# Feed-forward steps and next-sequence preparation moved half a slot to a slot later in hand-written engine orders

## The chip, the cores and the metric

The kernel runs on one core of one Trainium2 chip. A core has five engines that each work through their own list of instructions in order: PE (TensorE, matrix products and transposes), DVE (VectorE), ACT (ScalarE), POOL (GpSimd) and SP (SyncE, which here only issues transfers). Semaphores make an instruction wait for others, and what stands behind a waiting instruction on the same engine waits too. The metric is the device time of the execution in microseconds (us). Before the change it was 1479.51 us, the median of three runs (1479.34 to 1482.35).

## The reference

The input `x` is 8 sequences of 512 tokens with 256 features. The program is one transformer block:

```
x = x + layernorm(attention(layernorm(x)))
x = x + layernorm(ffn(layernorm(x)))
```

Attention has 16 query heads of width 128 in 4 groups; each group shares one key and one value head. Queries and keys get a sinusoidal position added; scores are causal and scaled by 1/sqrt(128); the heads' outputs are multiplied by `wo` (2048 x 256). The feed-forward part is a mixture of 64 experts (width 176). A token's gate scores are a softmax over 64 logits, its six best experts are taken, each expert takes at most 64 tokens in the order in which they come, and the outputs are summed with the scores as weights. A shared expert of width 352 is added for every token. All of it is fp32.

```
logits = x @ gate_w.T;  scores = softmax(logits);  topk_w, topk_idx = top_k(scores, 6)
g = silu(buf @ w_gate);  u = buf @ w_up;  d = (g * u) @ w_down        # per expert, 64 rows each
y = sum_k topk_w * d[...]  +  (silu(h @ sh_gate.T) * (h @ sh_up.T)) @ sh_down.T
```

## The kernel before

**Slots.** The main loop (from L903) runs over `k` from 0 to 127: sequence `b = k // 16`, head `s = k % 16`. One pass is called a slot here, "slot 4 of sequence 2" for `b = 2, s = 4`. The whole body runs under a manual schedule: every engine executes its instructions in the order in which the Python code emits them. A slot emits, in this order: the scores of head `k` (four row tiles, `scores`, each followed on DVE by a reduction called `least` that reads the score tile out of PSUM, and on ACT by an exponential); between the second and the third, `turned(k - 1)`, six DVE block transposes whose result goes through DRAM (`eb` to `ex_d` to `et`, issued by SP); then `weigh` (a DVE reciprocal, then four POOL multiplications of the softmax rows); place A; `project(k - 3)`; place B; `queries(k + 1)` (four PE pieces, and on DVE `qt`, which the next slot's scores need); `mix(k - 2)`; and place D.

**Places.** `side(s, place)` emits what a dictionary holds for that slot and place. The dictionary `behind` is filled at the end of slot 2 by `feed_forward(b - 1)`: it carries the second half of the block for the sequence just finished. Its steps that matter here are `copies` (attention output out of PSUM, ACT), `scales` (four `bn_stats`, four `bn_aggr`, one add on DVE, then a power on POOL), `residual_sums` (four DVE normalisations `o`, L106, then four POOL additions into `x`, L740), `store` (SP writes `x` to `x1_d`, L743), `rows` (four DVE normalisations into `xg`, L106), and `turn` (eight PE transposes `pt_f`, L119, whose two results are copied out by ACT and by DVE). Then come the shared expert (`shared_gate`, L681, with its DVE products L692 and L693) and the routing (`gate`, then `go("r")`: a reciprocal and eight small DVE operations, L392 to L398, in place D of slot 8).

**The next sequence.** `prepare(b + 1)` yields twelve units: the load of `x` (SP, L144), its scales, its normalisation `xn`, its transposes `pt_a` with the copies `xnt`, four `keys` units (PE `pk`, DVE `kt`) and four `values` units (PE `pv`, DVE add). One unit is emitted behind place D of a slot, and one slot has another just before `queries`.

**Buffers.** `ps_s` has three PSUM buffers, which score tiles and transposes (`psc`, `pt_f`, `pt_a`) take in turn; the fourth score tile takes the buffer of the first. Two transposes behind the scores of a slot take those of its second and third score tile, and the next slot's second and third score tile take the transposes'. `ps_m` has three for everything else. `x` has two buffers, so the load of sequence `b + 1` takes the one of sequence `b - 1`, which is free when `store` has landed and `rows` is done. `eb` has one.

**Experts.** Sequences 0 to 4 leave rows and gate scores in DRAM. From slot 14 of sequence 5 to about slot 4 of sequence 7 the generator `experts` (`routed`) runs the 32 pairs of experts between the attention steps: POOL gathers rows (`gx`, L513) and adds results into DRAM (`y_d`, L585), ACT's queue loads the weights (`wgu`, `wd`).

The places are called from these two lines, and nothing is reordered afterwards:

```
        def side(s, place):
            behind.pop(f"{s}{place}", lambda: None)()
```

Of the kernel before, what the change touches and what calls it, by code (L numbers as in the profile page):

```python
# [20 lines left out]
B, T, E = 8, 512, 256  # L21
# [18 lines left out]
EARLY = 5  # L40
# [4 lines left out]
def sandwich_kernel(ctx, tc, x, wq, bq_t, wkv, bk_t, bv, wo, gate_wt, w_gate, w_up, w_down,  # L45
# [26 lines left out]
    def norm_scales(tiles, name):  # L72

        n = len(tiles)
        st = small.tile([P, n, 6], F32, tag="st", name=f"st_{name}")
        for i in range(n):
            nc.vector.bn_stats(st[:, i, :], tiles[i])
        return scales_of(st, n, name)
# [20 lines left out]
    def tiles_of(t):  # L99
        return [t[:, i, :] for i in range(NI)]  # L100

    def rows_of(d, first):
        return d[first : first + T, :].rearrange("(i p) e -> p i e", p=P)

    def normalize(dst, src, mv, rs, i):
        nc.vector.tensor_scalar(dst, src, mv[:, i, 0:1], rs[:, i : i + 1], ALU.subtract, ALU.mult)  # L106
# [16 lines left out]
    with ExitStack() as part:  # L123
# [77 lines left out]
        turn = wpool.tile([1, NM], F32, tag="turn", name="turn")  # L201
# [70 lines left out]
        def queries(k):  # L272
            b, h = divmod(k, NH)
            pq = ps_m.tile([P, T], F32, tag="m", name=f"pq_{k}")
            for c in range(NC):
                nc.tensor.matmul(pq, lhsT=wq_sb[h // QPG][:, c, ts(h % QPG, D)], rhs=seqs[b]["xnt"][:, c, :],  # L276
                                 start=c == 0, stop=c == NC - 1)
            qt = p2.tile([D, T], F32, tag="qt", name=f"qt_{k}")
            nc.vector.scalar_tensor_tensor(qt, pq, bq_sb[:, h : h + 1], pe_sb, ALU.add, ALU.add)  # L279
            live[k] = {"qt": qt, "e": []}  # L280
# [383 lines left out]
        def residual(b, q, tag):  # L664
            x1 = q.tile([P, NI, E], F32, tag=tag, name=f"x1_{b}")
            nc.sync.dma_start(out=x1, in_=rows_of(x1_d, b * T))
            return x1
# [53 lines left out]
        def feed_forward(b):  # L721


            xt, sums = seqs[b]["x"], po.pop(b)
            l = {}

            def copies():
                l["o"] = p1.tile([P, NI, E], F32, tag="xn", name=f"o_{b}")
                for n in range(2):
                    nc.scalar.copy(l["o"][:, ts(n, 2), :], sums[n])  # L730

            def scales(src, name):
                l["scales"] = norm_scales(tiles_of(src), f"{name}{b}")

            def residual_sums():
                mv, rs = l.pop("scales")
                for i in range(NI):
                    normalize(l["o"][:, i, :], l["o"][:, i, :], mv, rs, i)
                for i in range(NI):
                    nc.gpsimd.tensor_add(xt[:, i, :], xt[:, i, :], l["o"][:, i, :])  # L740

            def store():
                nc.sync.dma_start(out=rows_of(x1_d, b * T), in_=xt)  # L743

            def rows():
                mv, rs = l.pop("scales")
                l["xg"] = p1.tile([P, NI, ROW], F32, tag="xg", name=f"xg_{b}")
                for i in range(NI):
                    normalize(l["xg"][:, i, :E], xt[:, i, :], mv, rs, i)

            def turn():
                l["xt2"] = p1.tile([P, NC, T], F32, tag="xt2", name=f"xt2_{b}")
                transpose_rows(l["xt2"], l["xg"], f"f{b}")

            def gate():
                l["r"] = route(b, l["xg"], l)
                next(l["r"])

            def shared_gate():
                l["f"] = shared(b, l["xt2"], l, "mmmmss" if b == B - 2 else "mmmmmm")  # L760
                next(l["f"])

            def go(which, n=1):
                return lambda: [next(l[which]) for _ in range(n)]

            steps = {
                "2D": copies, "3B": lambda: scales(l["o"], "o"), "3D": residual_sums,
                "4D": lambda: scales(xt, "f"), "5A": store, "5B": rows,
                "6A": turn, "7A": shared_gate, "7B": go("f"), "8A": gate,
                "8D": go("r"), "9D": go("r"),  # L770
            }
            if b < B - 2:
                steps |= {"9A": go("f"), "9B": go("f"), "11A": go("f"), "11B": go("f")}
            if b < EARLY:
                return steps | {"10A": go("r"), "10D": go("r", 2),
                                "11D": go("r", 2), "12A": go("f"), "12D": go("r", 2), "13A": go("f"), "13D": go("r", 2)}

            def mark():
                l["marks"] = marks(table["m"], l["xg"][:, :, E:ROW], table["places"], b, p1, "y")

            def gather_rows():
                gather("late", [(l["xg"], l["marks"][0])])
                l["gt"] = turn_scores(l.pop("marks")[1], b, *((p1, "xn") if b == EARLY else (p2, "kt", 5)))

            def begin_output():
                x1 = residual(b, p1, "xn") if b == EARLY else xt
                l["out"] = output(b, l["y"], x1)
                next(l["out"])

            def down_late():  # L790
                down("late")
                l["dd"] = pairs["late"]["dd"]

            steps |= {
                "10A": go("r"), "10B": mark, "10D": gather_rows, "11D": lambda: gate_up("late"),
                "12A": lambda: gate_up_hidden("late"), "12D": lambda: turn_hidden("late"), "13A": down_late,
            }
            if b < B - 2:
                return steps | {"13B": go("f"), "13D": lambda: [next(l["f"]), begin_output()],
                                "14B": go("out"), "15A": go("out")}  # L800

            steps["shared"], steps["output"] = go("f"), lambda: next(l["out"]) if "out" in l else begin_output()
            return steps
# [93 lines left out]
        behind, ahead = {}, iter(())  # L897
# [4 lines left out]
        def side(s, place):  # L902
            behind.pop(f"{s}{place}", lambda: None)()  # L903
            if not b:
                for u in rest.get(f"{s}{place}", ()):
                    u()

        for k in range(NK):
            b, s = divmod(k, NH)
            active = k >= EARLY * NH + 14  # L910
            scores(k, 0)
            scores(k, 1)
            if 0 <= k - 1 < NK - 2:
                turned(k - 1)
            if twice and not finishing:
                next(routed, None)
            scores(k, 2)
            scores(k, 3)
            if k == NK - 1:
                turned_at_once(k - 1)  # L920
            weigh(k)
            side(s, "A")
            if k >= 3:
                project(k - 3)
            side(s, "B")
            if active:
                next(routed, None)

            if s in ((8, 14) if b == EARLY + 1 else (7,)):
                next(ahead, lambda: None)()  # L930
            if k + 1 < NK:
                queries(k + 1)
            if k >= 2:
                mix(k - 2)
            if active and not finishing:
                next(routed, None)
            if not b:
                next(zeroing, None)
                next(zeroing, None)
            if k == FIRST_FREE:  # L940

                work = table["work"]
                table["rest"] = nc.values_load(work[0:1, 0:1], min_val=0, max_val=NM - 1)
                table["m"] = nc.values_load(work[0:1, 1:2], (ET.DVE, ET.SP), min_val=0, max_val=NM - 1)
                pairs["late"] = {"m": table["m"], "wgu_at": {"tag": "wgu_late", "bufs": 1},
                                 "wd_at": {"tag": "wd_late", "bufs": 1}}
                load_gate_up("late")
                load_down("late")
            if s == 2 and b:
                behind = feed_forward(b - 1)  # L950
            side(s, "D")
            if s == 5 and b + 1 < B:
                ahead = prepare(b + 1)
            u = next(ahead, None) if 5 <= s and (s != 6 or b != EARLY + 1) else None
            if u:
                u()
            twice = active and k > EARLY * NH + NH
            if twice and not finishing:
                next(routed, None)
            if active and not finishing and "all" in pairs:  # L960
                routed, finishing = finish_early(), True
# [90 lines left out]
```

## Time and profile before

The profiled execution took 1482.25 us. Its span, from the first to the last instruction of the program, is 1480.5 us, so 1.75 us lie around it. It is 2.74 us above the median of the timed runs.

| | |
|---|---|
| median of three runs | 1479.51 us |
| profiled execution, its span | 1482.25 us, 1480.5 us |
| PE busy | 1404.6 us (95%) |
| DVE, ACT, POOL busy | 887.2, 507.5, 424.8 us (60, 34, 29%) |
| first scores of sequences 1 to 7 | 158.8, 318.6, 478.6, 642.7, 802.6, 963.5, 1219.5 us |

A slot is taken from the first weight load of its scores to that of the next slot. In sequence 2, from the timeline of the weight loads:

| slot | 2 | 3 | 4 | 5 | 6 | 7 | 8 | 9 | 13 |
|---|---|---|---|---|---|---|---|---|---|
| start, us | 334.47 | 342.23 | 350.41 | 359.76 | 367.53 | 377.14 | 389.56 | 399.70 | 450.18 |
| length, us | 7.76 | 8.18 | 9.35 | 7.77 | 9.61 | 12.42 | 10.14 | 12.93 | 9.48 |

Slot 2 has only attention in it: 7.76 us of PE work without a gap. A unit of `keys` or `values` makes it 9.48 (1.72 more).

A line of the timeline gives the start and the duration in us, the engine, the source line, the operation with out<-in, the shape and the count of merged instructions; in square brackets stands how long the engine was idle just before, and whose result ended that. A line of the view of waits reads: who waited, for whom, us in total, number of times, longest.

### The profile page before, as it was taken

Reading aid. Unit: us, or ns where it says so; the run is one execution under the profiler, and the core shown is the slowest. Engines: PE = TensorE matmul, PEld = TensorE weight load, DVE = VectorE, ACT = ScalarE, POOL = GpSimd, SP = SyncE. Lnnn points to the kernel's source line nnn. Section 1 sums busy time; section 2 is a strip of 40 time slices with the busy share of each in tenths; the row PEclk is TensorE's granted clock in tenths of the full one; section 3 lists DMA queues with packets and bytes.
Section 4 is the critical chain, followed back from the end, with each engine's and each line's share of the span. In section 5 each row is a group of like instructions: output and inputs, shape, how many; then the busy total and the mean of one; then the engine's idle time right before and its main releaser. Section 6 shows DMA issues by size and latency. Waiting matters only on the chain. (4 is left out here: it accounts for less than half of the span.)

```text
span 1480.5 us, 18545 instructions
## 1 busy us (share of the span) xinstructions
PE 1404.6 (95%) x5310; PEld 853.3 (58%) x5310; DVE 887.2 (60%) x3094; ACT 507.5 (34%) x1450; POOL 424.8 (29%) x682
## 2 busy tenths in 40 slices
PE   9999999999999999999999999989899999899985
PEld 5656655666565655665566555655455655455553
DVE  5555576657655666557665766666455554567543
ACT  2333333233422333233323333233233243344432
POOL 2222231123211321123112411234434343523311
PEclk9999999999999999999999999999999999999998
DMA  7664554355444554445435554459999889668711
GB/s 257 195 181 142 156 169 144 105 158 163 150 132 131 160 153 137 121 152 168 142 107 157 162 151 136 132 184 252 253 236 242 240 232 255 179 194 259 211 47 62
DMA packets 160790, 252.03 MB, mean 170 GB/s; under 512 B 16412, under 2 KB 136189, under 8 KB 160685
## 3 DMA queue, kind: packets, MB, share of 16 engines
q1 hardware_dynamic: 131149, 206.76, 46.4%
q10 hardware_dynamic: 23392, 34.61, 8.6%
q0 software_dynamic: 6144, 9.44, 3.4%
q8 instruction: 44, 0.72, 0.2%
q14 instruction: 61, 0.50, 0.1%
HBM read 143.01 MB, written 107.74 MB: 169 GB/s over the span
## 5 line engine op out<-in xcount | busy, mean ns | idle before, releaser
L306 POOL TENSOR_SCALAR e<-e,recip 128x128 f32<-128x128 f32 x508 | 266.2, 557 | 802.6 <-DVE recip L303 775.1
L296 ACT ACTIVATE e<-e,least 128x128 f32<-128x128 f32 (+3 forms) x512 | 285.6, 559 | 388.9 <-DVE least L293 346.0
L289 PE MATMUL psc<-kt,qt 128*128 128x128 f32 (+3 forms) x1024 | 311.2, 441 | 24.3 <-DVE least L293 12.1
L349 PE MATMUL pav<-et,v 128*128 128x512 f32 (+3 forms) x1024 | 297.2, 433 | 5.3 <-ACT dd L584 5.3
L349 PEld LDWEIGHTS pav<-et,v 128*128 128x128 f32 x1024 | 194.0, 190 | 168.4 <-issue 117.9
L293 DVE CUSTOM_DVE_ANT_0 e<-psc,mask 128x128 f32<-128x128 f32 (+3 forms) x512 | 231.4, 478 | 52.1 <-PE psc L289 46.6
L361 PE MATMUL po<-wo_sb,ao 128*128 128x256 f32 x1024 | 243.5, 381 | 0.7 <-ACT ao L109 0.7
L276 PE MATMUL pq<-xnt,wq_sb 128*128 128x512 f32 x512 | 241.7, 594 | 1.0 <-ACT sc L388 0.7
L361 PEld LDWEIGHTS po<-wo_sb,ao 128*128 128x128 f32 x1024 | 192.5, 190 | 68.7 <-issue 37.4
L322 DVE STREAM_TRANSPOSE eb<-e 128x128 f32<-128x128 f32 x756 | 227.3, 364 | 4.0 <-DMA ex_d<-eb 4.0
L289 PEld LDWEIGHTS psc<-kt,qt 128*128 128x128 f32 x1024 | 166.0, 191 | 106.4 <-DVE least L293 37.7
L109 ACT COPY ao<-pav 128x512 f32<-128x512 f32 x128 | 75.0, 586 | 436.4 <-PE pav L349 416.5
L279 DVE SCALAR_TENSOR_TENSOR qt<-pq,bq_sb,pe_sb 128x512 f32<-128x512 f32 x128 | 95.7, 748 | 110.1 <-PE pq L276 110.1
L276 PEld LDWEIGHTS pq<-xnt,wq_sb 128*128 128x128 f32 x512 | 96.3, 191 | 71.9 <-issue 64.3
L303 DVE RECIPROCAL recip<-total 128x4 f32<-128x4 f32 x128 | 22.8, 178 | 126.8 <-ACT e L296 126.8
L296 ACT ACTIVATION_READ_ACCUMULATOR e<-e,least 128x1 f32 x512 | 95.7, 187 | 0.0
L585 POOL DMA_INDIRECT y_d<-dd,idx x32 | 50.9, 1591 | 113.4 <-DMA y_d<-dd,idx 80.3
L248 PE MATMUL pk<-xnt,wkv_sb 128*128 128x512 f32 x128 | 60.4, 594 | 0.2 <-ACT xnt L109 0.2
L259 PE MATMUL pv<-wkv_sb,xnt 128*128 128x512 f32 x128 | 60.2, 593 | 0.0
L261 DVE TENSOR_TENSOR v<-pv,bv_sb 128x512 f32<-128x512 f32 x32 | 22.1, 691 | 61.8 <-PE pv L259 61.8
L251 DVE SCALAR_TENSOR_TENSOR kt<-pk,bk_sb,pe_sb 128x512 f32<-128x512 f32 x32 | 24.0, 750 | 48.9 <-PE pk L248 48.9
L112 DVE COPY ht<-pth 88x256 f32<-88x256 f32 x32 | 13.4, 418 | 63.5 <-PE pth L566 63.4
(193 smaller groups left out, 1121.5 us busy)
## 6 DMA issues: line engine op xcount, KB each, us to landing
ex_d<-eb SPq DMA_DIRECT2D x126, 640.0 KB
et<-ex_d SPq DMA_DIRECT2D x504, 160.0 KB
wgu<-in_w_gate ACTq DMA_DIRECT2D x32, 352.0 KB
wgu<-in_w_up ACTq DMA_DIRECT2D x32, 352.0 KB
wd<-in_w_down ACTq DMA_DIRECT2D x32, 352.0 KB
y<-y_d SPq DMA_DIRECT2D x10, 512.0 KB
x<-in_x SPq DMA_DIRECT2D x8, 512.0 KB
x_d<-x SPq DMA_DIRECT2D x8, 512.0 KB
```

Of the source, the lines that this page charges most:

```text
L109: nc.scalar.copy(dst, src)
L248: nc.tensor.matmul(pk, lhsT=wkv_sb[:, c, g, 0, :], rhs=s["xnt"][:, c, :], start=c == 0, stop=c == NC - 1)
L259: nc.tensor.matmul(pv, lhsT=s["xnt"][:, c, ts(i, P)], rhs=wkv_sb[:, c, :, 1, :], start=c == 0, stop=c == NC - 1)
L276: nc.tensor.matmul(pq, lhsT=wq_sb[h // QPG][:, c, ts(h % QPG, D)], rhs=seqs[b]["xnt"][:, c, :], start=c == 0, stop=c == NC - 1)
L279: nc.vector.scalar_tensor_tensor(qt, pq, bq_sb[:, h : h + 1], pe_sb, ALU.add, ALU.add)
L289: nc.tensor.matmul(psc[:, :w], lhsT=l["qt"][:, ts(i, P)], rhs=seqs[b]["kt"][h // QPG][:, :w], start=True, stop=True)
L293: nc.vector.tensor_tensor_reduce(out=e, in0=psc[:, :w], in1=mask[:, T - w :], scale=-1.0 / math.sqrt(D), scalar=BIG, op0=ALU.add, op1=ALU. ...
L296: nc.scalar.activation(e, e, AF.Exp, bias=l["least"][:, i : i + 1], scale=-1.0, accum_out=l["total"][:, i : i + 1])
L306: engine.tensor_scalar(e, e, recip[:, n : n + 1], 1.0, ALU.mult, ALU.mult)
L322: nc.vector.transpose(blocks.rearrange("p c j t -> p j c t"), l["e"][i][:, js[0] * P : (js[-1] + 1) * P].rearrange("p (j c t) -> p j c t", ...
L349: nc.tensor.matmul(pav[:, :, j:, :], lhsT=seqs[b]["v"][:, j, ts(g, D)], rhs=l["et"][:, :, AT[j] : AT[j] + NI - j, :], start=j == 0, stop=j ...
L361: nc.tensor.matmul(po[b][i // 2][:, i % 2, :], lhsT=ao[:, ts(i, P)], rhs=wo_sb[:, h, :], start=h == 0 and i % 2 == 0, stop=h == NH - 1, sk ...
```

## The change

Nothing is added or removed; the number of instructions on each engine stays. Three things move.

- In `feed_forward`, `residual_sums` goes from 3D to 4A, the second `scales` from 4D to 5A, `store` from 5A to 5B, `rows` from 5B to 6A, and `turn` from 6A to a new place M of slot 6, which stands between `queries` and `mix`.
- The units of the next sequence start in slot 6 in place of 5, and the extra unit before `queries` is in slot 8 in place of 7. So the load of `x` is in slot 6, its scales in 7, `xn` and the transposes in 8, keys in 9 to 12, values in 13, 14 (two) and 15. In sequence 6 the scales are in 8, `xn` and the transposes in 9, and slot 10 has two keys.
- In sequence 6 the extra unit that stood before `queries` in slot 14 is now one of two at the end of that slot.

```diff
-                "2D": copies, "3B": lambda: scales(l["o"], "o"), "3D": residual_sums,
-                "4D": lambda: scales(xt, "f"), "5A": store, "5B": rows,
-                "6A": turn, "7A": shared_gate, "7B": go("f"), "8A": gate,
+                "2D": copies, "3B": lambda: scales(l["o"], "o"), "4A": residual_sums,
+                "5A": lambda: scales(xt, "f"), "5B": store, "6A": rows,
+                "6M": turn, "7A": shared_gate, "7B": go("f"), "8A": gate,
                 "8D": go("r"), "9D": go("r"),
...
-
-            if s in ((8, 14) if b == EARLY + 1 else (7,)):
+            if s == (9 if b == EARLY + 1 else 8):
                 next(ahead, lambda: None)()
             if k + 1 < NK:
                 queries(k + 1)
+            side(s, "M")
             if k >= 2:
                 mix(k - 2)
...
-            if s == 5 and b + 1 < B:
+            if s == 6 and b + 1 < B:
                 ahead = prepare(b + 1)
-            u = next(ahead, None) if 5 <= s and (s != 6 or b != EARLY + 1) else None
-            if u:
-                u()
+
+            for _ in range((0, 0, 0, 0, 0, 0, 1, 0, 1, 1, 2, 1, 1, 1, 2, 1)[s] if b == EARLY + 1 else
+                           (0, 0, 0, 0, 0, 0, 1, 1, 1, 1, 1, 1, 1, 1, 2, 1)[s]):
+                next(ahead, lambda: None)()
```

## The prediction

> **What bounds the kernel now.** I read the totals first.
>
> ```profile
> span 1480.5 us, 18545 instructions
> PE 1404.6 (95%) x5310; PEld 853.3 (58%) x5310; DVE 887.2 (60%) x3094; ACT 507.5 (34%) x1450; POOL 424.8 (29%) x682
> ```
>
> PE bounds it: only 1480.5 - 1404.6 = 75.9 us are without a matmul, 25 of them in the last slot and the tail. The change keeps all PE work, so it can only move the rest. The view of waits says who holds PE up, and, asked for SP's queue, that six loads of `x` stand behind the store of the buffer that they take:
>
> ```profile
> PE psc L289 <- DVE least L293: 12.1, 10, 2.5
> PE pt_f L119 <- DVE least L293: 6.1, 7, 1.4
> PE pgu L549 <- DVE gs L692: 3.7, 1, 3.7
> ```
>
> ```profile
> SPq L144 <- DMA x_d<-x: 29.1, 6, 7.3
> ```
>
> Third, the timeline of sequence 2, slots 3 to 6: first DVE, then PE.
>
> ```profile
> 349.62 0.74 DVE L279 SCALAR_TENSOR_TENSOR qt<-pq,bq_sb,pe_sb 128x512 f32<-128x512 f32 x1
> 350.85 2.19 DVE L106 TENSOR_SCALAR o<-o,mv_o,rs_o 128x256 f32<-128x256 f32 x4 [0.50 <-POOL rs_o L87]
> 352.97 0.28 DVE L293 CUSTOM_DVE_ANT_0 e<-psc,mask 128x128 f32<-128x128 f32 x1
> 364.99 1.84 DVE L106 TENSOR_SCALAR xg<-x,mv_f,rs_f 128x256 f32<-128x256 f32 x4
> 366.75 0.73 DVE L279 SCALAR_TENSOR_TENSOR qt<-pq,bq_sb,pe_sb 128x512 f32<-128x512 f32 x1
> ```
>
> ```profile
> 353.31 1.13 PE L289 MATMUL psc<-kt,qt 128*128 128x512 f32 x2 [1.33 <-DVE least L293]
> 371.16 0.66 PE L119 MATMUL pt_f<-ident,xg 128*128 128x128 f32 x4 [0.76 <-DVE least L293]
> ```
>
> In slot 3 the residual's normalisation `o` stands in front of the next slot's first `least`; PE's fourth score tile waits for that, and slot 4 takes 9.35 us for 7.76 of work. In slot 6 the second half of `pt_f` waits until DVE has emptied the third score tile. The same normalisation placed right behind the reciprocal (`xg`, slot 5) costs nothing: slot 5 takes 7.77.
>
> Last, two places where a late load of `x` reaches PE, in sequence 3 and in the expert stretch of sequence 6:
>
> ```profile
> 541.22 1.74 PE L289 MATMUL psc<-kt,qt 128*128 128x512 f32 x2 [2.53 <-DVE least L293]
> 542.75 3.01 PE L681 MATMUL psg<-xt,sg_sb 128*128 128x512 f32 x4
> 1059.18 2.62 PE L549 MATMUL pgu<-wgu,gxt 128*64 128x352 f32 x8 [3.74 <-DVE gs L692]
> ```
>
> What follows these waits is slow: `psg` 3.01 where 1.88 is usual, `pgu` 2.62 for 1.35.
>
> **What the Trainium skill says.** "TensorE: Matmul & The Clock Gate", section "HAM oscillation — how this bites in real kernels": idle gaps of PE beyond about 3.4 us make its clock drop. The trace agrees in kind, not in the figure: 2.53 us was enough, 2.68 in sequence 7 was not, and the 1.33 above did nothing. "SBUF — State Buffer", section "Who interferes with whom": a DVE operation with two ports and a POOL operation exclude each other for a whole instruction. The trace agrees: four normalisations take 1.37 us (`xn`, slot 7) when POOL rests, 1.84 beside POOL's softmax products, 2.19 beside its additions.
>
> **The change part by part**, times from a slot's start. In an unhindered slot the reciprocal starts at 5.13 (339.60 - 334.47), `qt` at 5.91, the next slot's first `least` at 7.76 + 0.53.
>
> Slot 4: `o` no longer stands behind `qt` of slot 3, and 4A has the position `rows` has in slot 5, with the same neighbours. 9.35 becomes 7.77: -1.58. POOL's additions (2.98) go behind its products of slot 4, which end at 7.6, and finish 2.8 into slot 5, before 5A reads them.
>
> Slot 5: 5A is where slot 3 has its first `scales` (statistics 1.37, aggregates 0.36, addition 0.57, then `qt` to 8.13). Slot 3 takes 8.18, so slot 5 goes from 7.77 to 8.18: +0.41. `store` at 5B is still behind the same SP transfers: 0.
>
> Slot 6: `rows` runs from 5.23 to 7.07 and the transposes that need it are in the same slot. PE would start them at 5.71 (mix's first matmul, 340.18 - 334.47). The fourth can start at 7.07 + 0.06 (signal, as `qt` to `psc`); from there four old `pt_f` pieces took 0.49 (371.16 to 371.65), five take 0.60: `mix` starts at 7.73 in place of 5.71. 7.76 + 2.02 = 9.78 against 9.61: +0.17. The `least` wait is gone, one on `xg` takes its place. Behind it wait `mix` and nothing else; `qt` is before the copy on DVE.
>
> Slot 7: the load of `x` is issued behind slot 6's `et` transfers, 7.9 into slot 6, with `store` landed; it has ten us until `scales` in 7D, against four. Today slot 7 takes 12.29, 12.42, 16.56, 12.31, 12.79 in sequences 1 to 5; work is 7.76 + 3.43 (shared expert, 379.34 to 382.77) + 0.87 (`pt_a`) = 12.06. Losses 0.23, 0.36, 4.50, 0.25, 0.73: 6.07, all removed. `scales` in 7D starts when `qt` is done (9.97), ends at 11.83; the next `least` is due at 11.72: no loss.
>
> Slot 8: loses a `keys` unit (1.72), gets `pt_a` (0.87), which 7 lost; slot 14 gets 1.72. Sum 0. The 0.31 that PE now waits for ACT's `xnt` go with it: -0.31.
>
> Slot 9: here is the price. DVE's order at the end of slot 8 is `xn`, `qt`, the eight routing operations, the copy `xnt`, `least`. Reciprocal to 5.27, gate maximum (0.40) to 5.62. `xn` meets POOL's products (unlike in slot 7), and having started in mid-piece takes about 2.0 (1.98 in slot 8 of sequence 6): 7.65. From `qt`'s start to the end of the routing was 2.55 (396.46 to 399.02): 10.20. Copy 0.69: 10.90. Slot 9 starts at 7.76 + 0.35 (`pg`) + 0.87 = 8.98; its third score tile needs the copied buffer, so its weights load at 10.95, 1.97 in. In old slot 8 that was 1.05 in (390.62 - 389.56) for a loss of 0.31; so the loss is 0.31 + 0.92 = +1.23. If `xn` takes 1.84 or 1.37: 0.96 or 0.5.
>
> Per sequence -1.58 + 0.41 + 0.17 - 0.31 + 1.23 = -0.08; five give -0.4. With slot 7: -6.5.
>
> Sequence 0 shifts its wait for `x` (1.6 on DVE) by a slot: 0.
>
> Sequence 6: `pt_f` comes behind expert work and finds `xg` done: -1.4. In slot 7 DVE waits 3.96 us for `ex_d<-eb`, because SP sat on the load of `x` until 1043.18; that is freed. ACT is held by weight loads until 1051.93, so `gs` comes 2 us earlier, not 4: -2 to -6.3 (3.97 wait and 2.3 of slow matmuls). Against it, DMA engines are 95 to 100% busy there and PE waits for `wd` in slot 8 (1.80): what is won may be waited for again. And POOL's additions (2.97) now stand ahead of one `gx` gather, issued at 1010.55, landing after 7.7, needed at 1021.9: the 3.65 to spare shrink to 0.7. From -7.7 to +3, I take -3.
>
> Sequence 7: slot 3's `o` holds the copy `ht` and PE for 1.78: gone. Slots 5 and 6 +0.41 + 0.17: -1.2.
>
> Sum: -6.5 - 3 - 1.2 = -10.7 from the profiled 1482.25: 1471.6. The timed runs lie at 1479.4 twice and 1482.35 once; the late load of sequence 3 (4.2 above its neighbours) is the kind of thing that differs. Without it: 1479.5 - 0.4 - 1.9 - 3 - 1.2 = 1473.0. I say 1472.5.
>
> **Rivals.** (1) The weight stream takes sequence 6's gain back: 1475.5. For it the DMA share; against it that ACT's and SP's queues, not bytes, ended the wait in slot 7. (2) The stream loses nothing and sequence 6 gives 7.7: 1468. (3) The new waits of slots 6 and 9 come out 0.7 more per sequence, and sequence 6 gives nothing: 1479, the same. Nothing excludes it; both rest on positions within a slot. (4) Slower: the wait at slot 9's third score tile grows past the point where the clock drops. It decides at about 2.5 us, 1.3 more than I have; then each sequence pays 1.3 + 1.7 (what slot 7 of sequence 3 lost beyond its wait) more, 15 us: 1487. Against it, 1.38 us of idleness in sequence 6 did nothing. It breaks even from 1.4 us per sequence. (5) That the change does nothing is excluded: the orders differ.
>
> **How the numbers follow.** Likeliest 0.44, (1) 0.14, (2) 0.06, (3) 0.2, (4) 0.16. The likeliest's own range is 1469 to 1476. No change is within 0.2%, 3 us, about what a measurement here can tell: 1476.5 to 1482.5. Faster 0.44 + 0.14 + 0.06 less a little that falls in the band: 0.61; same 0.22; slower 0.17. The range 1466 to 1482 leaves out (4) and some tails.
>
> **What would show it.** In sequences 1 to 5: slots 4, 5, 6, 7, 8, 9, 14 of 7.8, 8.2, 9.8, 11.2, 9.0, 14.2, 11.2. SP's wait of `x` for `x_d` (29.1) near 0; `pt_f` waiting for `xg`, not for `least`; slot 9's score tile waiting for the DVE copy `xnt`, five times about 1. In sequence 6, no wait of `eb` for `ex_d` in slot 7. I am wrong if slot 9 takes above 15, if matmuls behind the new waits run slow, or if sequence 6 (now 256.0 us) is not shorter.

## The result, and the profile after

The changed kernel takes 1467.18 us, the median of twelve runs (1461.01 to 1474.28), where the kernel before takes 1478.59 beside it (twelve runs, 1470.64 to 1484.6). The ratio is 0.993, with a 95% interval of 0.991 to 0.995: faster by 11.4 us, where 1472.5 was predicted and 1466 to 1482 was the range. The profiled execution took 1466.5 us, its span 1464.8.

The totals of the page after:

```profile
span 1464.8 us, 18561 instructions
PE 1405.2 (96%) x5310; PEld 854.5 (58%) x5310; DVE 890.4 (61%) x3094; ACT 509.7 (35%) x1450; POOL 427.8 (29%) x682
```

PE's work is what it was (1404.6 before). What shrank is the time without a matmul: 1464.8 - 1405.2 = 59.6 us in place of 75.9. The view of waits, PE's lines first and then the queue of SP for the load of `x` (who waited for whom, total us, times, longest; three dots stand for lines left out):

```profile
PE pd L575 <- DMA wd<-in_w_down: 8.0, 6, 2.9
PE pt_f L119 <- DVE xg L106: 7.6, 13, 5.1
...
PE psc L289 <- DVE xnt L112: 2.1, 5, 0.7
...
PE psc L289 <- DVE least L293: 1.6, 2, 1.3
```

```profile
SPq L144 <- DMA et<-ex_d: 1.4, 1, 1.4
...
SPq L144 <- DVE xt L112: 1.0, 3, 0.3
```

Six waits of 29.1 us for `x_d` are gone from SP. `psc` waits 1.6 us for `least` where it was 12.1, and `pt_f` no longer waits for `least` at all. New are the waits of `pt_f` for `xg` (one of 5.1 was there before, the other twelve come to 2.5 us) and of `psc` for `xnt`. The wait for the experts' weights `wd` grew from 5.8 to 8.0.

The timeline of sequence 2, DVE and then PE (start, duration, what; in brackets the idle time just before and who ended it). Slot 4 begins at 348.23, slot 6 at 364.19, slot 8 at 385.16, slot 9 at 394.38:

```profile
353.45 1.85 DVE L106 TENSOR_SCALAR o<-o,mv_o,rs_o 128x256 f32<-128x256 f32 x4
...
356.54 0.29 DVE L293 CUSTOM_DVE_ANT_0 e<-psc,mask 128x128 f32<-128x128 f32 x1 [0.58 <-PE psc L289]
...
390.70 2.19 DVE L106 TENSOR_SCALAR xn<-x,mv_a,rs_a 128x256 f32<-128x256 f32 x4
...
395.34 0.67 DVE L112 COPY xnt<-pt_a 128x512 f32<-128x512 f32 x1
```

```profile
371.31 0.77 PE L119 MATMUL pt_f<-ident,xg 128*128 128x128 f32 x5 [0.26 <-DVE xg L106]
...
394.49 1.21 PE L289 MATMUL psc<-kt,qt 128*128 128x128 f32 x4
396.07 1.77 PE L289 MATMUL psc<-kt,qt 128*128 128x384 f32 x4 [0.37 <-DVE xnt L112]
397.68 1.88 PE L681 MATMUL psg<-xt,sg_sb 128*128 128x512 f32 x4
```

In slot 4 the normalisation `o` now stands ahead of `qt` (355.22), and DVE waits 0.58 us for the next scores in place of being late for them. In slot 8 `qt` starts at 392.80, behind `xn`, and the routing fills the time from there to the copy. In slots 6 and 9 PE has the two new waits, and `psg` behind the second runs at its usual 1.88.

Slot lengths in sequences 1 to 5, from the weight loads of the scores, beside those of before and the predicted ones:

| slot | 4 | 5 | 6 | 7 | 8 | 9 | 14 |
|---|---|---|---|---|---|---|---|
| before | 9.35 | 7.77 | 9.61 | 12.29 to 16.56 | 10.14 | 12.93 | 9.48 |
| predicted | 7.8 | 8.2 | 9.8 | 11.2 | 9.0 | 14.2 | 11.2 |
| after | 7.77 | 8.19 | 9.78 | 11.19 | 9.22 | 13.62 | 11.19 |

After the change they repeat to 0.02 us in all five, but for slot 9 of sequence 3 (13.90) and slot 14 of sequence 5, where the expert work starts (11.65; 9.93 before). So the slots are a far sharper measure than the total, whose runs spread over 13 us. By sequence (0, 1 to 5, 6, 7) the pair of profiles gives 141.2, 804.7, 256.0, 261.0 before and 139.7, 797.0, 254.5, 256.1 after. The profiled pair differs by 15.7 us and the medians by 11.4, so some of what the pair shows in sequences 6 and 7 is chance; experiments below take that apart.

### The profile page after: what moved, and what is told of

It reads as the page before. It is cut to its first block, busy times and chain, and to the rows that moved or that the text cites. A ratio compares the mean times of both kernels' runs of the same rounds, so it can differ in the third digit from the quotient of the medians.

```text
span 1464.8 us, 18561 instructions
## 1 busy us (share of the span) xinstructions
PE 1405.2 (96%) x5310; PEld 854.5 (58%) x5310; DVE 890.4 (61%) x3094; ACT 509.7 (35%) x1450; POOL 427.8 (29%) x682
## 5 line engine op out<-in xcount | busy, mean ns | idle before, releaser
L306 POOL TENSOR_SCALAR e<-e,recip 128x128 f32<-128x128 f32 x508 | 271.7, 578 | 788.8 <-DVE recip L303 760.6
L296 ACT ACTIVATION_READ_ACCUMULATOR e<-e,least 128x1 f32 x512 | 95.7, 187 | 0.0
```

The costliest lines, as they stand in the source:

```text
L296: nc.scalar.activation(e, e, AF.Exp, bias=l["least"][:, i : i + 1], scale=-1.0, accum_out=l["total"][:, i : i + 1])
L306: engine.tensor_scalar(e, e, recip[:, n : n + 1], 1.0, ALU.mult, ALU.mult)
```

## The experiments

**My theory** was that in sequences 1 to 5 the gain comes from the load of `x`, which no longer reaches PE late in slot 7, that the edits of slots 4 to 9 about cancel, and that sequence 6 adds some 3 us because SP is freed. The rivals: the new waits are dearer, the weight stream takes sequence 6's gain back, or the clock drops behind the longer waits.

Each experiment gives the median in us, then its ratio to the kernel before, run beside it, with the 95% interval. The edits are shortened to the entries that change.

**1. The units alone.** The changed kernel with the feed-forward steps put back:

```diff
-"3B": scales(o), "4A": residual_sums, "5A": scales(xt), "5B": store, "6A": rows, "6M": turn
+"3B": scales(o), "3D": residual_sums, "4D": scales(xt), "5A": store, "5B": rows, "6A": turn
```

> Only the units of the next sequence move a slot later; the feed-forward steps stay where they were before the change. Theory A (each slot is set by what stands in front of it in DVE's order, and the moves add up): in sequences 1 to 5 slots 4, 5 and 6 stay at 9.35, 7.77 and 9.61 us, slots 7, 8, 9, 14 take the lengths of the whole change (11.19, 9.22, 13.62, 11.19), and SP's wait of the load of x for the store of x goes to near 0. That leaves about 8 us of the 11 to the feed-forward moves: about 1475 us. Theory B (the gain is the late load of x alone): about the time of the whole change, 1467 to 1469 us.

Measured: 1476.03 us, ratio 0.999 (0.9975 to 1.0005). Slots 4, 5, 6 are back at 9.35, 7.77, 9.61, and slots 7, 8, 9, 14 stay at 11.19, 9.22, 13.61, 11.19; SP waits for no `x_d`. The two groups of edits don't touch each other's slots. Sequences 1 to 5 take 802.0 us, against 798.8 for experiment 2, which removes the late load without moving a unit: the moved units cost 0.6 per sequence, over what changes place between slots 7, 8, 9 and 14. In the median the units alone gain nothing that can be told from chance; the feed-forward steps take off the other 5.0 us of sequences 1 to 5.

**2. The store alone.** The kernel before, with nothing changed but `store`, half a slot earlier:

```diff
-"4D": scales(xt), "5A": store
+"4D": scales(xt) and store
```

> The kernel before, with one edit: the store of x moves from place A of slot 5 to place D of slot 4, some 8 us earlier on SP, so that it has landed when the load of x takes its buffer. Nothing on the other engines is moved. Theory A: slots 4, 6, 8 stay at 9.35, 9.61, 10.14; SP's wait of 29.1 us for the store goes to below 5; slot 7 of sequences 1 to 5 comes to about 12.1 (0.3 for each, and 4 where a load was late), and slot 7 of sequence 6 loses its wait of the block transposes for the transfer before: 3 to 7 us in all, about 1473 us. Theory B (the late load is the whole gain): 1467 to 1469 us.

Measured: 1471.25 us, ratio 0.9943 (0.9918 to 0.9968), between the two expectations. SP's waits for the load of `x`:

```profile
SPq L144 <- DMA et<-ex_d: 3.5, 1, 3.5
...
SPq L144 <- DVE least L293: 1.3, 4, 0.4
```

The 29.1 us for `x_d` are gone here too. Slot 7 is 12.07 in all five sequences, which is the 12.06 of work that the prediction counted, and slots 4, 6 and 8 are untouched. The late load was worth 804.7 - 798.8 = 5.9 us in sequences 1 to 5 of these profiles (predicted 6.07), and the median is 6.3 us under that of the kernel before beside it (1477.56): one line gives over half of what the whole change gives. The profile before had one very late load, in sequence 3; that of experiment 10, where sequences 1 to 5 are those of before, takes 803.5, which makes it 4.7.

**3. The transposes ahead of the queries.** The changed kernel with `turn` right behind `rows`:

```diff
-"6A": rows, "6M": turn
+"6A": rows and turn
```

> The whole change, but the transposes of the rows stand directly behind the normalisation in place A of slot 6, ahead of project and queries, not behind the queries. Theory A: PE stands still from 2.2 us into the slot until the normalisation is done at 7.07, project, queries and mix come after it, and the wait is long enough for slow matmuls behind it: slot 6 takes 13 to 15 us in place of 9.78 in sequences 1 to 5, and the whole about 1490 us. Theory B (the place behind the queries is worth little, since nothing but the wait moves): slot 6 at most 10.5, the whole within 3 us of 1467.

Measured: 1500.01 us, ratio 1.016 (1.0122 to 1.0197); slot 6 takes 15.59, 14.89, 14.71, 14.40, 14.38 in sequences 1 to 5 and 16.0 in sequence 7, which the expectation of 1490 had left out. Slot 6 of sequence 1, PE:

```profile
211.37 2.79 PE L119 MATMUL pt_f<-ident,xg 128*128 128x128 f32 x8 [3.23 <-DVE xg L106]
213.95 3.62 PE L361 MATMUL po<-wo_sb,ao 128*128 128x256 f32 x8
```

PE waits 3.23 us, and then `pt_f` takes 2.79 where eight such transposes (`pt_a`) take 1.04, and `po` 3.62 for 1.89. Place M is what makes `rows` at 6A affordable: between the two places stand `project` and `queries`, which PE can do while DVE normalises.

**4. The transposes behind mix.**

```diff
-"6M": turn
+"6D": turn
```

> The whole change, but the transposes of the rows go one step further, from between queries and mix to the end of slot 6, behind mix. Theory A: the normalised rows are done by then, so slot 6 is 7.76 + 0.87 = 8.63 us in place of 9.78; the two copies of the transposes then stand close to the next slot's scores, which costs slot 7 the 0.31 us that it cost slot 8 before the change: 0.84 us less per sequence, about 5 us in all, 1462 us. Theory C (the copies in front of the next slot's scores cost what is won): slot 7 at 12.3 or more, the whole at 1467 us.

Measured: 1465.0 us, ratio 0.9912 (0.9885 to 0.9938). Slot 6 is 8.63 and slot 7 is 11.59, together 20.22 where the changed kernel has 20.97: the 0.48 us of idleness in slot 6 are gone, and 0.75 per sequence with them.

**5. The routing later.** In the changed kernel the eight routing operations go behind the next slot's softmax:

```diff
-"8D": go("r"), "9A": go("f")
+"9A": go("r") and go("f")
```

> The changed kernel with the routing of slot 8 (a reciprocal and eight small DVE operations) moved from place D of slot 8 to place A of slot 9, so that it no longer stands between qt and the copy xnt. Theory A (slot 9 loses time because its third score tile waits for the copy of pt_a, and the routing is what makes the copy late): slots 8 and 9 together 22.84 -> about 22.46 in sequences 1 to 5, slot 9 13.62 -> about 13.24, PE's wait of psc for xnt gone; about 1465 us. Rival B (DVE has too little room in slot 9: the routing delays qt and the products there): slot 9 stays at 13.6 or above; 1467 us or more.

Measured: 1465.68 us, ratio 0.9917 (0.9889 to 0.9946). Slot 9 is 12.99 in all five sequences (13.24 was expected), slot 8 stays at 9.22. So the routing ahead of the copy `xnt` costs the changed kernel 13.62 - 12.99 = 0.63 us per sequence. The 13.90 of sequence 3 goes as well.

**6. The statistics behind mix.**

```diff
-"3B": scales(o), "5A": scales(xt)
+"3D": scales(o), "5D": scales(xt)
```

> The changed kernel with both scales (of o and of x) moved behind mix: from 3B to 3D and from 5A to 5D; store stays in 5B. Theory A (slots 3 and 5 are 0.42 longer than an empty slot because the 2.3 us of statistics stand ahead of qt on DVE): slots 3 and 5 8.18 and 8.19 -> 7.76 to 7.85, -0.83 per sequence, about 1462 us. Rival B (behind qt they stand ahead of the next slot's first least, as the normalisation o did in slot 3 of the kernel before): slots 4 and 6 become longer by 0.4 or more each, no gain or a loss, 1467 to 1472 us.

Measured: 1460.43 us, ratio 0.9887 (0.986 to 0.9914). Slots 3 and 5 are 7.76 and 7.75, an empty slot's length (-0.86 per sequence), and slots 4 and 6 stay at 7.77 and 9.77. Rival B falls, and DVE's timeline of slot 3 of sequence 2 (from 339.60) shows why:

```profile
345.49 0.75 DVE L279 SCALAR_TENSOR_TENSOR qt<-pq,bq_sb,pe_sb 128x512 f32<-128x512 f32 x1 [0.61 <-PE pq L276]
346.16 1.39 DVE L77 BATCH_NORM_STATS2 st_o<-o 128x6 f32<-128x256 f32 x4
...
347.94 0.28 DVE L293 CUSTOM_DVE_ANT_0 e<-psc,mask 128x128 f32<-128x128 f32 x1
```

`qt` is done 6.6 into the slot, and the statistics just fill the time until the next slot's first `least`, which starts 8.34 in, where 8.29 is when it is due without them. In the kernel before, slot 3 held the statistics ahead of `qt` and the normalisation `o` behind it: DVE had one slot's spare time for two such pieces.

**7. The last three together** (edits 4, 5 and 6).

> The changed kernel with three moves together: the transposes of rows behind mix (6D), the routing at 9A, both scales behind mix (3D, 5D). Theory A (each move takes away its own wait, so they add): -0.75 - 0.38 - 0.83 = -2.0 per sequence, with the changed kernel's 7.7 some -9.6 per sequence 1 to 5 against before; about 1456 us, ratio to the kernel before about 0.985. Rival B (a move only pushes the wait to the next slot, where another of them stands): 1461 to 1465 us, with slots 6 and 7 together still above 20.2 or slot 4 above 8.2.

Measured: 1455.36 us (1453.16 to 1460.17), ratio 0.9845 (0.9818 to 0.9873). Sequences 1 to 5 take 157.0 us each (157.5 the fifth), 785.6 in all, 11.5 less than in the changed kernel; the three alone give 5 x (0.75 + 0.63 + 0.86) and the 0.28 of sequence 3, which is 11.5. The savings add, since each removes its own wait; 0.24 us per sequence are left without a matmul. This is the best version here: it beats the kernel before by 22.5 us in the medians. What still waits is in sequences 6 and 7; PE's three longest totals are 5.3 us for `wd`, 5.2 for ACT's `dd` and 5.1 for `xg` near the end.

**8. A longer wait.** The changed kernel with work added: four more `bn_stats`, whose result nothing uses, between the routing and the copy `xnt` in slot 8.

```diff
+for i in range(NI): nc.vector.bn_stats(more[:, i, :], l["xg"][:, i, :E])    # 8D, behind go("r")
```

> The changed kernel with added work: four more bn_stats of xg on DVE (1.37 us, their result is not used) in place D of slot 8 between the routing and the copy xnt, which lengthens the wait of slot 9's third score tile by about 1.4 us. It tests the case that a longer wait there makes the matmuls behind it slow. Theory A (only the wait grows, PE's clock holds): slot 9 13.62 -> about 15.0, wait for xnt about 1.9 more in total than today each, 1474 us. Rival B (matmuls behind an idle time of that size run slow): slot 9 16.5 or above, 1482 us or more.

Measured: 1476.71 us, ratio 0.9999 (0.9983 to 1.0015), more than theory A's 1474 and short of B's 1482. The profile shows theory A in four sequences and B in one. Slot 9 takes 14.91 in sequences 1, 2, 4 and 5, and 16.89 in sequence 3. PE in sequence 2, then in sequence 3:

```profile
400.50 1.77 PE L289 MATMUL psc<-kt,qt 128*128 128x384 f32 x4 [1.68 <-DVE xnt L112]
402.10 1.88 PE L681 MATMUL psg<-xt,sg_sb 128*128 128x512 f32 x4
...
561.31 1.97 PE L289 MATMUL psc<-kt,qt 128*128 128x384 f32 x4 [1.95 <-DVE xnt L112]
563.07 3.42 PE L681 MATMUL psg<-xt,sg_sb 128*128 128x512 f32 x4
```

The same instructions, in the same place: after a wait of 1.68 us `psg` takes 1.88, after one of 1.95 it takes 3.42. A quarter of a microsecond more of waiting costs 16.89 - 14.91 = 1.98 us; the last section says what decides.

**9 to 11. Sequences 6 and 7.** (`b` in `feed_forward` is the sequence just finished, so its work in sequence 6 has `b == EARLY`, which is 5.) The first kernel gives the changed kernel's sequence 6 the places of the kernel before (steps and units), the second gives the kernel before the changed kernel's places in sequence 6 alone, and the third gives the changed kernel's sequence 7 the feed-forward places of before. The changed kernel ran again beside the first two. The number of units in each slot of sequence 6 goes with the places and is not shown in the edit.

```diff
+if b == EARLY:      # the third: EARLY + 1; the second the other way round, in the kernel before
+    steps: "3D": residual_sums, "4D": scales(xt), "5A": store, "5B": rows, "6A": turn
-            if s == (9 if b == EARLY + 1 else 8):
+            if s in ((8, 14) if b == EARLY + 1 else (8,)):
-            if s == 6 and b + 1 < B:
+            if s == (5 if b == EARLY + 1 else 6) and b + 1 < B:
```

> The changed kernel, but sequence 6 has the places of the kernel before: its feed-forward steps at 3D, 4D, 5A, 5B, 6A, its units of the next sequence from slot 5. Theory A (the prediction's step: the change wins about 3 us in sequence 6): about 3 us slower than the changed kernel of the same call, about 1470 us, and the wait of eb for ex_d in slot 7 is back. Rival B (the weight stream takes the gain back, sequence 6 gives nothing): within 1 us of the changed kernel. In both, sequences 1 to 5 keep the changed kernel's slots (159.3 us each).

> The changed kernel as it is, in the same call as the two others: 1465 to 1469 us, ratio to the kernel before 0.993. Sequences 1 to 5 repeat 159.3 us each to 0.3; what differs from its first profile is in sequences 6 and 7.

> The kernel before, but sequence 6 has the places of the changed kernel. Theory A (3 us won in sequence 6): 3 us faster than the kernel before, about 1475 us, ratio 0.998. Rival B (nothing is won there): within 1 us of the kernel before, about 1478 us, ratio 1.000. In both, sequences 1 to 5 keep the slots of the kernel before, SP's wait of x for x_d is there five times in place of six, and the wait of eb for ex_d in slot 7 of sequence 6 is gone.

> The changed kernel, but sequence 7 has the feed-forward places of the kernel before (3D, 4D, 5A, 5B, 6A); it has no units of a next sequence. Theory A (the prediction's step: 1.2 us won in sequence 7, of which slot 4 gives 1.78 and slots 5 and 6 take 0.58 back): about 1.2 us slower than the changed kernel, 1468.5 us, slot 4 of sequence 7 11.0 in place of 9.09, slots 5 and 6 7.8 and 9.6. Rival B (what the first pair of profiles showed, 4.9 us, comes from the change there): about 5 us slower, 1472 us. In both, sequences 1 to 5 take 159.3 us each.

| kernel | median, us | ratio to before (95%) | seq. 1 to 5 | seq. 6 | seq. 7 |
|---|---|---|---|---|---|
| changed, again | 1467.51 | 0.9936 (0.9918 to 0.9954) | 796.9 | 254.4 | 256.1 |
| changed, sequence 6 as before | 1468.94 | 0.9953 (0.9934 to 0.9972) | 797.0 | 252.9 | 257.5 |
| before, sequence 6 as changed | 1477.42 | 0.9998 (0.9987 to 1.0009) | 803.5 | 255.7 | 259.7 |
| changed, sequence 7 as before | 1469.07 | 0.9944 (0.9928 to 0.996) | 796.9 | 251.1 | 257.2 |

Sequence 6's edits are worth 1.4 us in one direction (2.5 by the ratios) and 0.6 (0.3) in the other. The first, with six executions of each kernel, can't tell nothing from 3 us; the interval of the second, 0.9987 to 1.0009 from 22 executions, leaves out the 0.998 of theory A. So rival B holds, or nearly. SP's waits moved as expected: with the places of before it waits 7.4 us for `x_d` once more, and with the changed ones five times in place of six. The profiled length doesn't follow the places: 252.9 and 256.0 with those of before, 251.1 to 255.7 with the changed ones in this table. Nor does the sum of its slots 6 to 10, where the edits act: 96.6 and 92.1 with the places of before, 94.3, 92.6, 95.7 and 92.0 with the changed ones.

Sequence 7's edits come to 1 to 2 us (1469.07 against 1467.51 and 1467.18; 1.2 and 2.1 by the ratios), so the 4.9 of the first pair is not theirs alone. Slot 4 there is 10.80 in place of 9.09, as expected; slots 5 and 6 go to 7.78 and 9.62 from 8.84 and 9.78.

Where sequence 6 loses its gain, the slots of all the profiles show. (Experiment 3, whose slot 6 is another, is left out.)

| feed-forward places of sequence 6 | slot 6 | slot 7 | slot 8 |
|---|---|---|---|
| of before (before, experiments 1, 9, and 2 with its `store`) | 16.2 | 21.0 to 23.6 | 17.8 to 19.6 |
| changed (both profiles, experiments 4 to 8, 10, 11) | 14.6 to 15.4 | 17.4 to 19.7 | 20.0 to 25.1 |

The means of slot 7 differ by 3.6 us, those of slot 8 by 3.0 the other way, though slot 8 has 0.87 us of transposes less. In slot 8 of the changed places PE stands without a matmul for 4.0 to 7.0 us, with those of before for 1.8 to 2.6; in seven of the nine profiles 2.1 to 2.9 of it are a wait for the weights `wd`. From the changed kernel's timelines of DVE and PE and its table of stretches:

```profile
1063.72 1.81 DVE L322 STREAM_TRANSPOSE eb<-e 128x128 f32<-128x128 f32 x6 [6.00 <-DMA ex_d<-eb]
```

```profile
1063.95 1.97 PE L575 MATMUL pd<-wd,ht 88*64 88x256 f32 x8 [2.88 <-DMA wd<-in_w_down]
```

```profile
1055.98:1077.75 21.77, 17.72 (x74) 9.17 (x73) 11.46 (x45) 7.90 (x26) 9.13 (x10) 0.84 0.93 261
```

(Stretch and length, busy us of PE, PEld, DVE, ACT, POOL, then the granted clock, the DMA share and GB/s. The stretch is slot 8; slots 6 and 7 have a clock of 1.00.) The wait of `eb` for `ex_d`, 3.96 us in slot 7 before (2.20 in experiment 9), is now 6.00 in slot 8 (3.66 in the changed kernel's second profile, 5.35 in experiment 10). SP's queue shows where it comes from; the lines are from its timeline, first of before, then of after (the start is the issue):

```profile
1043.18 0.40 SPq L144 DMA_DIRECT2D x<-in_x  x1
1043.69 0.44 SPq L326 DMA_DIRECT2D ex_d<-eb  x1
1051.85 1.75 SPq L329 DMA_DIRECT2D et<-ex_d  x4
```

```profile
1044.62 0.35 SPq L530 DMA_DIRECT2D wd_late<-in_w_down  x1
1046.43 0.39 SPq L144 DMA_DIRECT2D x<-in_x  x1
1046.99 0.37 SPq L326 DMA_DIRECT2D ex_d<-eb  x1
1063.68 1.75 SPq L329 DMA_DIRECT2D et<-ex_d  x4
```

`et` is issued when `ex_d` has landed. Before, that took 1051.85 - 1043.69 = 8.2 us behind the 512 KB of `x`, and 8.5 in the next slot behind the three loads for the late experts (`wgu_late` twice and `wd_late`, 352 KB each). The change puts `x` right behind these, and `et` follows at 1063.68, 16.7 us after `ex_d`. In the eleven profiles with the two loads in a row it takes 11.1 to 16.7, in the three with them apart (before, experiments 2 and 9) 7.6 to 10.7.

But neither the two loads in a row nor SP's wait sets the length of the slots. In experiment 1 the loads stand in a row too (12.7), and yet `eb` waits for nothing in slots 6 to 10, and slot 8 takes 18.83. In experiment 2 `x` is sent early and apart from the weights, and `eb` waits for nothing there either; but PE still waits 2.21 us for `gs` in slot 7 (2.63 in experiment 1; 1.99 in experiment 9, where `eb` does wait), and slots 6 to 10 take 93.5, between the 92.1 and 96.6 that they take with the waits. What the feed-forward steps win in slot 7, PE waits for in slot 8. That the weights' arrival sets the pace is read from the wait for `wd` and the busy DMA engines; a run with less of the weight stream was not made.

## Why the prediction was right, and where it was not

**Right in its main step, which it then made too small.** The late load was counted at 6.07 us, and the store alone, with no other edit, gives 5.9 in the slots and 6.3 in the median. For the timed runs, though, the prediction kept 1.9 of the 6.07, because the 4.2 of sequence 3 looked like chance. Sequence 3 does differ from run to run (4.50 lost before, 1.87 in the profile of experiment 10), but so do the others: that profile loses 0.4 to 1.3 in each of them, and 4.7 in all. That is the largest part of the distance between the gain of about 7 us that 1472.5 stands for and the 11.4 measured. Slots 4, 5, 6, 7 and 14 came out within 0.03 of the working.

**Slots 8 and 9: right in the order, 0.3 too dear.** DVE's order was followed rightly: `qt` was to start 7.65 into slot 8 and started at 392.80 - 385.16 = 7.64; the copy was to end at 10.90 and ended at 395.34 + 0.67 - 385.16 = 10.85. But slot 8 is the empty slot, `pt_a` and 0.59, not 0.35, around `pg`; it is 9.22 in place of 8.98, also when the routing is moved. So slot 9 starts 0.24 later, and its third score tile waits less. The two steps "-0.31" and "+1.23" can be measured at the matmuls. In slot 8 before:

```profile
389.67 2.72 PE L289 MATMUL psc<-kt,qt 128*128 128x128 f32 x8
392.32 0.46 PE L382 MATMUL pg<-ident,lg 64*128 64x64 f32 x4
```

From `psc` to `pg` it is 2.65 there and 2.25 after: the old wait cost 0.40, not 0.31. From `psc` to `psg` in slot 9 it is 397.68 - 394.49 = 3.19 after and 2.18 before (400.13 to 402.31): the new one costs 1.01, not 1.23. Net that is +0.61, and the table has +0.62, in place of +0.92. (The table splits it as -0.07 and +0.69: before, the `keys` unit in slot 8 lets the first weights of slot 9 be loaded 0.43 ahead of their matmul, without it 0.11, which moves the border between the two slots by 0.3.) A sequence gains 0.37 by its edits and not 0.08; five of them 1.5 us more than predicted. With the 6.07 that is 7.9; 7.7 was measured. The page "SBUF — State Buffer" of the Trainium skill, section "Who interferes with whom", which the prediction used for `xn` beside POOL, fits again: `xn` took 2.19 there (2.0 was taken), against 1.37 with POOL at rest.

**Sequence 0: counted as 0, it gives 1.5 in the pair.** The wait was not shifted by a slot but mostly lost: slots 7 and 8 go from 9.97 + 9.55 to 7.76 + 8.63, and slot 14 takes 1.71 of that back as moved work. It returns in part by chance; in the profile of experiment 11 slot 8 of sequence 0 is 10.77, with 1.63 us idle.

**Sequence 6: the step that failed.** The prediction took -3: 1.4 from `pt_f`, and at least 2 from SP, which is "freed" when the load of `x` no longer waits. The first came: PE's 1.38 for `least` before `pt_f` is gone, and slot 6 shrinks by 0.8 to 1.6. The second did not. Experiment 2 frees SP, and the wait for `gs` is 2.21 with no wait of `eb`, as it is 1.99 with one in experiment 9. When the feed-forward steps move, slot 7 does get 3.6 us shorter, and slot 8 gives 3.0 of it back in waits for weights. So the argument against the first rival, that "ACT's and SP's queues, not bytes, ended the wait in slot 7", looked at one slot too few. The prediction had named this itself ("what is won may be waited for again"). It also followed the load of `x` past `et` and the store, but not to the three late weight loads in its new slot, behind which `eb` now waits for `ex_d`. The edits of this sequence measured 0.6 and 1.4 us (0.3 and 2.5 by the ratios), not 3.

**Sequence 7: right in kind.** Slot 4 gave 1.93 in the pair (1.71 against experiment 11) for the 1.78 counted; slot 5 cost 1.06, not 0.41. What else differs in its expert part changes from run to run, and how much of it the edits cause is open.

**The rivals.** (1) was right that sequence 6 would keep little, and the waits for `wd` in slot 8 fit its mechanism; its 1475.5 was still too high because of the late load, slots 8 and 9 and sequence 0. (3) is out: the new waits came out 0.3 cheaper per sequence. (4) did not happen: in the changed kernel's profile the clock is full until 988.5 us, in sequence 6. But its price was placed wrongly. It was to decide at 2.5 us of waiting; experiment 8 shows the drop between 1.68 and 1.95 in that very place. From the 0.37 that PE waits there in the changed kernel that leaves 1.3 to 1.6 us, about what was thought, but from the 1.23 that the prediction took as the wait it would have left only 0.5 to 0.7. The chance of 0.16 for it was not too high.

So the 11.4 us of the medians are about 6.4 to 7.8 from sequences 1 to 5 (803.5 and 804.7 against 796.9 and 797.0), 1.1 to 1.5 from sequence 0 (141.2 against 140.1 and 139.7), and the rest from sequences 6 and 7 with some chance in it.

## What to carry to other kernels

When a transfer waits for another one, look first at the one line that issues the earlier of the two: here half a slot on `store` is worth more than half of the whole change. In an order written by hand, put long DVE steps where the next instruction that needs DVE is itself still waiting for something else, and take each moved step's own new wait as a separate price, since such prices add (0.75, 0.63 and 0.86 per sequence here). And where a stretch waits for the memory, price a removed wait over the next slot too: in sequence 6 slot 7 got 3.6 us shorter and slot 8 3.0 longer. When a transfer is moved, list also what is already queued in its new slot: behind two loads in a row `ex_d` landed 11.1 to 16.7 us after its issue, behind either alone after 7.6 to 10.7.

## What the runs showed of the hardware

- What makes PE's clock drop is its idle time within fixed stretches of 3.41 us, not the length of a wait. Each trace records when the granted clock changes. In each of the 14 traces all these moments lie whole multiples of 3.41 us apart, and the clock is either full or half. PE's idle time, by the trace's ends of the matmuls, can be summed in every stretch of this grid, from 20 to 1458 us of each trace. Of 5800 stretches at full clock, 77 had more than 1.92 us of idleness, and half clock followed all of them; 5706 had less than 1.78, and it followed none; the 17 in between went both ways. From the tables of stretches of experiment 8 (slot 9 of sequences 2 and 3) and of before (a wait of 2.68 in sequence 7; columns as above, the clock is the third number from the end):

```profile
398.91:402.32 3.41, 1.82 (x5) 1.06 (x6) 3.41 (x14) 0.98 (x4) 0.00 (x0) 1.00 0.00 0
402.32:405.74 3.42, 3.42 (x9) 1.52 (x8) 2.18 (x8) 1.91 (x5) 0.74 (x2) 1.00 0.47 192
559.34:562.75 3.41, 1.46 (x5) 0.87 (x5) 3.41 (x14) 0.99 (x4) 0.00 (x0) 1.00 0.02 5
562.75:566.16 3.41, 3.41 (x5) 1.35 (x4) 2.02 (x8) 1.43 (x4) 0.35 (x2) 0.50 0.47 192
```

```profile
1258.40:1261.81 3.41, 2.15 (x8) 0.84 (x6) 1.57 (x4) 0.00 (x0) 0.00 (x0) 1.00 0.70 252
1261.81:1265.23 3.42, 2.00 (x6) 1.24 (x7) 0.67 (x2) 1.26 (x3) 2.34 (x4) 1.00 0.48 126
1265.23:1268.64 3.41, 3.41 (x25) 1.99 (x24) 0.36 (x2) 1.56 (x3) 1.31 (x3) 1.00 1.10 268
```

The 1.95 us fell into one stretch, and the clock of the next was halved; of the 1.68, 1.59 were in one stretch. The 2.68 were parted into 1.26 and 1.42 and did nothing, where the 2.53 of sequence 3 fell into one (538.18 to 541.60). So whether a wait of that size costs anything depends on where it falls. The Trainium skill, "TensorE: Matmul & The Clock Gate", section "HAM oscillation — how this bites in real kernels", puts the gap at about 3.4 us; here little more than half of it is enough.
- The same wait can cost a different amount each time: the drop behind the 3.2 us of experiment 3 makes slot 6 15.59 in sequence 1 and 14.38 in sequence 5, with 3.36 to 3.71 us of idleness in each of sequences 1 to 5. In sequence 1 the clock stays at half for two stretches (6.83 us), in sequences 2 to 5 for one.
